# A graph network's layer-1 tables, made block by block beside layer 0's edge loop

## Chip, cores and metric

One core of one Trainium2 chip. The metric is the device time of one execution in microseconds; the kernel before took 9594.02 us, the median of three runs.

## What is computed

Four graph layers with residuals on 12500 nodes of 128 features and 200000 edges. dst is sorted; it is drawn as 12500 u², so low nodes have most of the edges. h is the rectified layer norm of x ahead of every layer.

```python
# layer 0: attention over incoming edges and a self loop, at dst
h = h @ W; e = leaky_relu(a_s[src] + a_d[dst])
x = x + segment_sum(h[src] * softmax_by_dst(e), dst)
# layer 1: 8 heads, at src
q, k, v = h @ Wq.T + bq, h @ Wk.T + bk, h @ Wv.T + bv
a = (dot(q[src], k[dst]) / 4 + mlp(edge_weight1)) * cutoff(edge_weight1)
x = x + layernorm(h + segment_sum(softmax_by_src(a) * v[dst], src) @ Wo.T + bo)
# layer 2: both directions, normed by degree; layer 3: mean over dst, batch norm
```

## The kernel before

The nodes are 98 blocks of 128. Edges are handled 128 to a tile; a row gather (`gather`, L340, an indirect DMA issued by GpSimd) fetches one table row for each of a tile's edges, and a one-hot matrix product adds the rows to the sums in SBUF (`acc`, one row of 137 columns per node). There are four stages of gathers: `hw` (layer 0), `kvt` (layer 1), `zt` (layer 2), `h` (layer 3).

`layer0_edges` is unrolled in 196 steps. A step takes two windows of four tiles: eight gathers, then the weights of the edges (L1346 to L1358), the weighted one-hot matrices on ScalarE and VectorE (L1365 to L1368), four matmuls per window (L1372), and two additions per window into the two blocks that a window can touch (L1375). Because dst is sorted, low blocks are complete long before the loop ends. A generator, `background`, is advanced once a step, and twice in every sixteenth: it loads layer 1's weights and then sorts the edges by source (`sort`; L484 to L497 are its exchanges, L518 to L529 its turns through PE).

After the loop, the sorted keys are stored to DRAM, `layer0_wide` stands as a loop that runs 0 times or once (a test of the data, read into a register by every engine, decides; it doesn't run here), and then comes the stage between the layers. It works in seven chunks of 14 blocks: `layer0_out` divides by the sums and adds x (L1463), `layernorm_stats` takes statistics (L313), the result goes to DRAM (`xd`), `layer1_table` makes keys, values and queries (a rectified norm L329, a transpose L777, its copy L779, two matmuls of 384 columns L1476 and L1477, three copies out L1478 to L1480) and stores them (`kvt`, `qd`). Between chunks `source_tiles` makes layer 1's lists: for each tile the indices, places and lengths of its edges, with 2 + 13 + 13 gathers from the sorted keys (`edge`, `keyt`, `far`), unpacking on VectorE (L442 to L449) and 39 transposes (L1221). `cutoff` follows. All kvt rows must be in DRAM before layer 1's first gather.

Layer 1's loop (`attention`) has its order written out by hand, as a pipeline over groups of eight tiles. Layer 2 (`layer2_edges`) mixes gathers with sums by buckets of edges, which need the array `bucketp`, loaded by `bucket_places`. Elsewhere the framework's scheduler chooses each engine's order ahead of time; engines then run in that order and wait on semaphores.

```python
for lo, hi in groups(c0, c1):
    net.layer1_table(work, psum2, kv_view, q_view, rows0, lo, hi, ln)
nc.gpsimd.memset(acc[:, c0:c1, :], 0.0)
for _ in range(2):
    next(fill, None)
```

Of the kernel before, what the change touches and what calls it, by code (L numbers as in the profile page):

```python
# [37 lines left out]
P = 128  # L38
# [19 lines left out]
G = 4  # L58
# [40 lines left out]
CHUNKS = [(b, b + CHUNK) for b in range(0, NB, CHUNK)]  # L99

# [17 lines left out]
class Net:  # L118
# [773 lines left out]
    def bucket_places(self, pool, places, over):  # L892

        nc = self.nc
        place = pool.tile([P, BC, P], F32, name="bucketp")
        nc.sync.dma_start(place, places)
        none = pool.tile([P, 1], F32, name="bnone")
        nc.vector.tensor_scalar(none, over, -4096.0, None, op0=OP.mult)
        nc.vector.tensor_scalar(place, place, none, None, op0=OP.add)
        return place.rearrange("p c b -> p (c b)")  # L900

    def buckets(self, work, psum, table, lanes, place, finish, classes=CLASSES, zb=ZB):
# [15 lines left out]
        for k0 in range(0, classes, n):  # L918
            cols = COLS[k0 // FEW]
            sums = [psum.tile([P, 512], F32, name=f"sums{i}", bufs=1)[:, :cols] for i in range(n)]  # L920
            for s in range(NB):
# [10 lines left out]
                for i in range(0, n, 2):  # L932
                    p = psum.tile([P, 2, PARTS * D], F32, name="pout", bufs=2)
                    yours = work.tile([P, 2, COLS[classes > FEW]], F16, name="yours", bufs=4 + (zb == ZB))[:, :, :cols]
                    for j in range(2):
                        b = s * CLASSES + k0 + i + j
                        nc.tensor.matmul(p[:, j, :], mine[:, (i + j) * P:(i + j + 1) * P], z[:, s % zb, :],  # L937
                                         start=True, stop=True)
                        nc.vector.tensor_scalar(yours[:, j, :], self.iotac[:, :cols], place[:, b:b + 1], None,  # L939
                                                op0=OP.is_equal)  # L940
# [57 lines left out]
    def windows(self, pool, psum, dram, lists, own, other, rel, size, count, lanes):  # L998
# [9 lines left out]
        ownf = pool.tile([P, RC, P], F32, name="ownf")  # L1008
# [22 lines left out]
        for i, e in enumerate((P - 1, (E - 1) % P)):  # L1031
# [4 lines left out]
        some = pool.tile([P, 2], F32, name="somefar")  # L1036
# [4 lines left out]
                                       self.ident[:, last % P:last % P + 1], op0=OP.is_ge, op1=OP.mult)  # L1041
        p = self.bank(psum)
        nc.tensor.matmul(p[:, 0:2], self.ones, some, start=True, stop=True)
        nc.vector.tensor_scalar(self.found[size], p[:, 0:2], 0.5, None, op0=OP.is_gt)

        nc.vector.tensor_sub(rel, ownf, base[:, :, None].to_broadcast([P, RC, P]))
        otherf = pool.tile([P, RC, P], F32, name="otherf")
# [37 lines left out]
    def source_tiles(self, pool, psum, dram, lists, keys, shifted, values, firsts, lanes, lengths):  # L1085
# [9 lines left out]
        idx, place, void, length, oblocks, obases = lists  # L1095
# [5 lines left out]
        f = small("firsts", R)  # L1101
# [32 lines left out]
        below = small("below", R, BF16)  # L1134
# [60 lines left out]
        key = pool.tile([P, RC, P], I32, name="keyt")  # L1195
        far = pool.tile([P, RC, P], F32, name="far")
# [8 lines left out]
        own, other, rest = (pool.tile([P, RC, P], I32, name=f"{n}t") for n in ("own", "other", "rest"))  # L1205
# [6 lines left out]
        short = pool.tile([P, RC, P], F16, name="shortt")  # L1212
# [3 lines left out]
        for c0 in range(0, RC, 4):  # L1216
            n = min(4, RC - c0)
            for i, (t, out) in enumerate(((otherf, idx), (rel, place), (far, length))):
# [8 lines left out]
            yield  # L1227
        nc.vector.tensor_scalar(void, place, float(P), -1e30, op0=OP.is_ge, op1=OP.mult)
        yield

    def source_pairs(self, pool, key, sown, sother):

        nc = self.nc
        keys, own, other, more = (pool.tile([P, RC, P], I32, name=f"{n}p") for n in ("key", "own", "other", "more"))
        nc.vector.memset(keys[:, RC - 1, :], 0)
        self.load_rows(keys, key)
        self.unpack_buckets(own, other, more, keys)
        self.store_rows(sown, own)
        self.store_rows(sother, other)
        first = pool.tile([P, RC], F32, name="firstp")  # L1240
        nc.vector.memset(first, float(NOWHERE))
        whole = R - (RC - 1) * P
        nc.vector.tensor_copy(first[:, :RC - 1], own[:, :RC - 1, 0])
        nc.vector.tensor_copy(first[:whole, RC - 1:], own[:whole, RC - 1, 0:1])
        return sown, sother, first
# [79 lines left out]
    def layer0_edges(self, acc, lists, background):  # L1325
        nc, tc = self.nc, self.tc
        idx, place, mask, blocks, bases = lists
        n = D + 2
        with tc.tile_pool(name="l02", bufs=1) as work, tc.tile_pool(name="ps02", bufs=2, space=PSUM) as psum:
            self.banks = 2  # L1330
            steps = background(psum)
            for s in range(-(-NW // 2)):
                lo, two = s * W, min(2, NW - 2 * s)
                m = two * G
                rows = work.tile([P, W, ROW], F32, name="rows", bufs=5)
                for j in range(m):
                    self.gather(rows[:, j, :], self.hw, idx, lo + j)
                lane = work.tile([P, W * P], BF16, name="lanes", bufs=3)
                nc.sync.dma_start(lane[:, :m * P], self.rows(self.dlanes[lo:lo + m, :], m * P))
                near = work.tile([P, 2, 3], BF16, name="near", bufs=4)  # L1340
                for i, v in enumerate(self.blocks_of(bases, 2 * s, two, [SP], NP - P - 1)):
                    nc.sync.dma_start(near[:, i, :], self.tb[bass.ds(v, P), :])
                b = self.blocks_of(blocks, 2 * s, two, [DVE], NB - 2)

                mine = work.tile([P, W, P], BF16, name="mine", bufs=2)
                nc.vector.tensor_scalar(mine.rearrange("p g e -> p (g e)")[:, :m * P], lane[:, :m * P], self.lane, None,  # L1346
                                        op0=OP.is_equal)
                pt = psum.tile([P, W, 3], F32, name="pt")
                for j in range(m):
                    nc.tensor.matmul(pt[:, j, :], mine[:, j, :], near[:, j // G, :], start=True, stop=True)  # L1350
                w = work.tile([P, W], F32, name="weight", bufs=3)
                nc.vector.tensor_reduce(w[:, :m], pt[:, :m, :], axis=AX.X, op=OP.add)
                nc.vector.tensor_mul(w[:, :m], w[:, :m], rows[:, :m, D + 2])
                nc.vector.tensor_max(w[:, :m], w[:, :m], rows[:, :m, D + 3])
                minus = work.tile([P, W], F32, name="minus", bufs=3)
                nc.vector.tensor_scalar(minus[:, :m], w[:, :m], -1.0, None, op0=OP.mult)  # L1356

                nc.vector.reciprocal(rows[:, :m, D + 1], w[:, :m])  # L1358
                hot = work.tile([P, W, P], F32, name="weights", bufs=2)
                for j in range(m):  # L1360
                    at = place[:, lo + j:lo + j + 1]
                    if j % G < 3:

                        off = work.tile([P, P], BF16, name="off", bufs=8)
                        nc.scalar.activation(off, self.iotab, AF.Abs, bias=at, scale=-1.0)  # L1365
                        nc.scalar.activation(hot[:, j, :], off, AF.Relu, bias=w[:, j:j + 1], scale=minus[:, j:j + 1])  # L1366
                    else:
                        nc.vector.tensor_scalar(hot[:, j, :], self.iota, at, w[:, j:j + 1], op0=OP.is_equal, op1=OP.mult)  # L1368
                for i in range(two):
                    p = psum.tile([P, n], F32, name="psum", bufs=2)  # L1370
                    for j in range(i * G, i * G + G):
                        nc.tensor.matmul(p, hot[:, j, :], rows[:, j, :n], start=j % G == 0, stop=j % G == G - 1)  # L1372
                    d = acc[:, bass.ds(b[i], 2), :n]
                    for h in range(2):
                        nc.vector.scalar_tensor_tensor(d[:, h, :], p, mask[:, 2 * s + i, h:h + 1], d[:, h, :], op0=OP.mult,  # L1375
                                                       op1=OP.add)
                next(steps, None)
                if s % 16 == 8:
                    next(steps, None)
            for _ in steps:  # L1380
                pass
            self.banks = 1
# [74 lines left out]
    def layer0_out(self, acc, rden, x, lo, hi):  # L1457
# [3 lines left out]
        nc.vector.reciprocal(rden[:, lo:hi], acc[:, lo:hi, D])  # L1461
        for b in range(lo, hi):
            nc.vector.scalar_tensor_tensor(acc[:, b, :D], acc[:, b, :D], rden[:, b:b + 1], x[:, b - lo, :],  # L1463
                                           op0=OP.mult, op1=OP.add)

    def layer1_table(self, work, psum, kv_view, q_view, x, lo, hi, ln):

        nc = self.nc  # L1470
        kv = work.tile([P, 4, 2 * D], F32, name="kv", bufs=2)
        q = work.tile([P, 4, 2, D], F16, name="qparts", bufs=2)
        ht = self.normed_transposed(work, psum, x, lo, hi, ln)
# [908 lines left out]
```

## Time and profile before

| | us |
|---|---|
| timed runs, median (lowest, highest) | 9594.02 (9591.22, 9601.5) |
| profiled execution, its own time | 7967.66 |
| its span | 7965.0 |
| layer 0's edge loop, first to last gather | 196.4 to 2168.1 |
| layer 1's gathers begin | 2346.4 |
| layer 2's gathers begin | 4750.8 |
| layer 3's gathers begin | 7048.7 |
| mean granted TensorE clock | 0.759 |

The profile is of one execution. Its time is shorter than that of the timed runs; the profile does not say why. A group's line gives the line of code, the engine, the operation, what is written from what, the shapes and the count; then the busy time and the mean duration in ns; then the idle time ahead of it on its engine, and what ended most of that. A window's line gives each engine's busy time in a stretch.

### The profile page before, as it was taken

The numbers are of one execution on the slowest core, as the hardware profiler recorded it, in microseconds if no ns is written. First come the engines' busy times: TensorE is split into PE (matmuls) and PEld (weight loads), VectorE is DVE, ScalarE is ACT, GpSimd is POOL, SyncE is SP. The second block draws the span as 40 slices with busy tenths as digits, with TensorE's granted clock in tenths as the row PEclk, the third lists the DMA queues.
The fourth block names the chain that finished last, engine by engine and source line by source line (L and its number), as shares of the span: only waits on it lengthen the run. The fifth ranks groups of instructions, "written<-read, shape, count | busy, mean of one in ns | idle before, by whom it ended". The sixth has DMA issues, their size and how long they took to land. (4 is left out here: it accounts for less than half of the span.)

```text
span 7965.0 us, 123010 instructions
## 1 busy us (share of the span) xinstructions
PE 5216.0 (65%) x36039; PEld 4233.1 (53%) x36040; DVE 5606.0 (70%) x17675; ACT 3772.7 (47%) x8051; POOL 5505.8 (69%) x5641
## 2 busy tenths in 40 slices
PE   4344544444376666666666537776888898768887
PEld 3344444444346666656666536555644554456665
DVE  5687777777667776666666666666766776778887
ACT  4466666666463333223333364443534454456556
POOL 0777777777637777777777557777777766357774
PEclk7566666656586667677676669888988998879999
DMA  6333333333475555555556514443433443445554
GB/s 107 85 83 82 79 83 80 84 79 82 94 222 186 186 185 175 174 175 172 183 179 189 137 61 135 133 127 118 149 115 118 125 132 117 109 120 135 150 150 122
DMA packets 780792, 1038.72 MB, mean 130 GB/s; under 512 B 202181, under 2 KB 548698, under 8 KB 779834
## 3 DMA queue, kind: packets, MB, share of 16 engines
q1 hardware_dynamic: 535039, 543.32, 23.2%
q0 software_dynamic: 202304, 471.89, 22.1%
q10 hardware_dynamic: 42747, 15.32, 0.9%
q8 instruction: 298, 4.88, 0.2%
q14 instruction: 404, 3.31, 0.1%
HBM read 963.63 MB, written 66.40 MB: 129 GB/s over the span
## 5 line engine op out<-in xcount | busy, mean ns | idle before, releaser
L942 ACT ACTIVATE r<-pout 128x512 f16<-128x512 f32 x2352 | 1400.2, 597 | 1268.9 <-PE pout L937 1144.7
L340 POOL DMA_INDIRECT rows<-hw,idxd x1564 | 1492.5, 954 | 674.1 <-issue 449.0
L340 POOL DMA_INDIRECT rows<-zt,idxs x1624 | 1560.0, 961 | 559.2 <-issue 405.0
L340 POOL DMA_INDIRECT rows<-kvt,idxs x1624 | 1591.3, 980 | 494.9 <-issue 418.5
L914 PE MATMUL sums<-yours,r 128*128 128x288 f16 (+1 forms) x9408 | 1875.9, 323 | 3.2 <-DVE yours L939 2.8
L939 DVE TENSOR_SCALAR yours<-iotac,bucketp 128x288 f16<-128x288 f16 (+1 forms) x4704 | 1351.0, 329 | 311.8 <-PE sums L914 286.1
L1372 PE MATMUL psum<-rows,weights 128*128 128x130 f32 x3128 | 731.6, 415 | 638.0 <-ACT weights L1366 526.9
L914 PEld LDWEIGHTS <-r 128*128 128x128 f16 x9408 | 944.5, 101 | 338.5 <-issue 7.0
L1372 PEld LDWEIGHTS psum<-rows,weights 128*128 128x128 f32 x3128 | 658.0, 311 | 676.6 <-ACT weights L1366 587.7
L937 PE MATMUL pout<-z,mine 128*128 128x256 f16 x4704 | 930.3, 281 | 39.2 <-ACT r L942 35.7
L340 POOL DMA_INDIRECT rows<-h,late x620 | 606.8, 979 | 185.4 <-issue 145.5
L1602 ACT ACTIVATE weighted<-lg 128x64 f32<-128x64 f32 x203 | 53.1, 262 | 1438.5 <-DVE lg L1600 1438.5
L1623 PE MATMUL psum<-weighted,hot 128*128 128x137 f32 x3136 | 662.6, 391 | 74.4 <-DVE weighted L1612 73.8
L1596 DVE TENSOR_TENSOR rows<-pq,rows 128x512 f32<-128x512 f32 x406 | 280.5, 691 | 571.0 <-DMA rows<-kvt,idxs 570.4
L1623 PEld LDWEIGHTS psum<-weighted,hot 128*128 128x128 f32 x3136 | 622.4, 290 | 98.6 <-DVE weighted L1612 95.2
L1366 ACT ACTIVATE weights<-off,weight,minus 128x128 f32<-128x128 bf16 x1173 | 483.6, 481 | 336.8 <-DVE minus L1356 202.5
L1583 PE MATMUL pq<-query,mine 128*128 128x128 f16 x3136 | 333.7, 291 | 467.5 <-DVE mine L1552 464.7
L1872 PE MATMUL psum<-rows,hot 128*128 128x128 f16 x3248 | 341.8, 232 | 411.8 <-DMA rows<-zt,idxs 367.4
L937 PEld LDWEIGHTS <-mine 128*128 128x128 f16 x4704 | 450.1, 101 | 272.9 <-issue 54.6
L1583 PEld LDWEIGHTS <-mine 128*128 128x128 f16 x3248 | 306.1, 137 | 498.7 <-DVE mine L1552 495.5
L1870 DVE TENSOR_SCALAR hot<-iotac,places 128x128 f16<-128x128 f16 x1624 | 367.6, 281 | 280.4 <-PE psum L1872 279.1
L1872 PEld LDWEIGHTS <-hot 128*128 128x128 f16 x3248 | 249.8, 103 | 528.9 <-issue 475.0
(497 smaller groups left out, 9240.7 us busy)
## 6 DMA issues: line engine op xcount, KB each, us to landing
near<-lengths SPq DMA_DIRECT2D x203, 512.0 KB
lanes<-lanes SPq DMA_DIRECT2D x112, 896.0 KB
lanes<-slanest SPq DMA_DIRECT2D x203, 256.0 KB
z<-zt SPq DMA_DIRECT2D x112, 448.0 KB
lanes<-lanes SPq DMA_DIRECT2D x196, 256.0 KB
lanes<-dlanes SPq DMA_DIRECT2D x195, 256.0 KB
rows<-kvt,idxs POOLq DMA_INDIRECT x1624
rows<-zt,idxs POOLq DMA_INDIRECT x1624
```

What stands on the lines that cost most here:

```text
L340: self.nc.gpsimd.indirect_dma_start(out=out, out_offset=None, in_=table, in_offset=bass.IndirectOffsetOnAxis(ap=idx[:, t:t + 1], axis=0))
L914: nc.tensor.matmul(sums[i], self.part(r[:, i, :], h), yours[:, i, :], start=s == 0 and h == 0, stop=s == NB - 1 and h == PARTS - 1)
L937: nc.tensor.matmul(p[:, j, :], mine[:, (i + j) * P:(i + j + 1) * P], z[:, s % zb, :], start=True, stop=True)
L939: nc.vector.tensor_scalar(yours[:, j, :], self.iotac[:, :cols], place[:, b:b + 1], None, op0=OP.is_equal)
L942: nc.scalar.activation(r, p, AF.Copy)
L1366: nc.scalar.activation(hot[:, j, :], off, AF.Relu, bias=w[:, j:j + 1], scale=minus[:, j:j + 1])
L1372: nc.tensor.matmul(p, hot[:, j, :], rows[:, j, :n], start=j % G == 0, stop=j % G == G - 1)
L1583: nc.tensor.matmul(pq[:, j, :], s["mine"][i][:, j, :], s["query"][i * G + j][:, h * D:(h + 1) * D], start=h == 0, stop=h == 1)
L1596: nc.vector.tensor_mul(k, s["pq"][i], k)
L1623: nc.tensor.matmul(p, s["hot"][j // G][:, j % G, :], v[:, j, :], start=first and j == 0, stop=last and j == W - 1)
L1870: nc.vector.tensor_scalar(hot, self.iotac[:, :P], place[:, lo + j:lo + j + 1], None, op0=OP.is_equal)
L1872: nc.tensor.matmul(p, hot, self.part(rows[:, j, :], h), start=first and h == 0, stop=last and h == PARTS - 1)
```

## The change

- `layer0_out`, `layer1_table` and the chunk loop between the layers become one generator, `layer1_tables`, in chunks of seven blocks (the last two of four and three). `layer0_edges` calls `prep(s)` at the end of every step; it advances the generator by up to two pieces (three once `background` is used up), if `after_step` says that the chunk's blocks are complete by that step. What is left runs after the loop. acc is no longer cleared afterwards, and x + layer 0's output stands in the chunk's own tile.
- A test in `windows` compares, for each chunk but the last, the first dst of the row at which the chunk is due with the chunk's end. If some block is late (`soon`), a loop after layer 0 makes all tables again; it runs 0 times or once.
- `background` goes on after the sort with the stores of the keys, `source_tiles` and `cutoff`, and is advanced a second time in every sixth step instead of every sixteenth.
- Memory: five SBUF buffers of 128 x 1664 (`bufs`) serve in turn the edge arrays, the sort, the lists, and later `bucketp`. In `layer0_edges` the small product `pt` has four places in one PSUM bank (two banks before), the two windows' products share one bank in each of two buffers (one bank each before), and the tables get one bank (`prep`). In `attention`, `near` has three buffers instead of four and is loaded three groups ahead instead of four; `weighted` has two instead of three.

```diff
+STEP = 7
+PREP = [(b, b + STEP) for b in range(0, NB - STEP, STEP)] + [(NB - STEP, NB - 3), (NB - 3, NB)]
+def after_step(hi):
+    return min(-(-NW // 2), int(NW * math.sqrt(min(1.0, hi * P / N)) / 2) + 2)
...
+        for i, (_, hi) in enumerate(PREP):
+            row = min(2 * after_step(hi), NW) * G
+            if hi == NB or row >= NW * G:
+                nc.vector.memset(some[:, 2 + i:3 + i], 0.0)
+            else:
+                nc.vector.scalar_tensor_tensor(some[:, 2 + i:3 + i], ownf[:, row // P, 0:1], float(hi * P),
+                                               self.ident[:, row % P:row % P + 1], op0=OP.is_lt, op1=OP.mult)
...
-                pt = psum.tile([P, W, 3], F32, name="pt")
+            pt = pts[:, s % 4]
...
-                    p = psum.tile([P, n], F32, name="psum", bufs=2)
+            p = psum.tile([P, 2, n], F32, name="psum", bufs=2)
...
-                if s % 16 == 8:
-                    next(steps, None)
+            if next(steps, self) is self or s % 6 == 1 and next(steps, self) is self:
+                self.banks = 1
+            prep(s)
...
+    def layer1_tables(self, work, psum, acc, ln, views):
+        for c0, c1 in PREP:
+            yield c1
+            k = c1 - c0
+            x = work.tile([P, STEP, D], F32, name="x", bufs=2)[:, :k]
+            self.load_x(x, c0, c1)
+            rden = work.tile([P, STEP], F32, name="rden", bufs=2)[:, :k]
+            nc.vector.reciprocal(rden, acc[:, c0:c1, D])
+            for b in range(k):
+                nc.vector.scalar_tensor_tensor(x[:, b, :], acc[:, c0 + b, :D], rden[:, b:b + 1], x[:, b, :],
+                                               op0=OP.mult, op1=OP.add)
+                if b % 3 == 2:
+                    yield c1
+            nc.scalar.dma_start(xd_view[:, c0:c1, :], x)
+            self.layernorm_stats(work, ln, c0, c1, x)
+            yield c1
+            for lo in range(0, k, 4):
...
+                for j in range(n):
+                    p = bank()[:, :3 * D]
+                    nc.tensor.matmul(p, self.onesb, self.parts, start=True, stop=False)
+                    nc.tensor.matmul(p, ht[:, j, :], self.qkv, start=False, stop=True)
+                    nc.scalar.activation(q[:, j, 0, :], p[:, :D], AF.Copy)
+                    nc.vector.tensor_sub(q[:, j, 1, :], p[:, :D], q[:, j, 0, :])
+                    nc.scalar.activation(kv[:, j, :], p[:, D:], AF.Copy)
+                    if j % 2:
+                        yield c1
...
+        yield from net.source_tiles(sort_pool, psum, bufs, short, oblocks, obases, skeys[:R, :], shifted, shiftedl,
+                                    firsts, net.by_tile[1], net.by_tile[0])
+        net.cutoff(flat[2], flat[4].bitcast(I32), flat[1])
...
+        def prep(s):
+            for _ in range(2 + (net.banks == 1)):
+                if due and s >= after_step(due[0]) and due[0] < NB:
+                    due[:] = [v for v in [next(tables, None)] if v is not None]
...
+    nc.vector.tensor_max(wide, wide, net.soon)
+    once = net.count_of(dlist, wide, 1)
+    with tc.tile_pool(name="l1t", bufs=1) as work, tc.tile_pool(name="ps10", bufs=1, space=PSUM) as psum, \
+            tc.For_i(0, once, 1):
+        for _ in net.layer1_tables(work, psum, acc, ln, views):
+            pass
```

## The prediction

> **What bounds the kernel now.** I read the page first, then busy time by stage, then GpSimd's timeline where layer 0 ends, then groups of instructions and waits. The page has a group that repeats in all four layers, the row gathers on GpSimd:
>
> ```profile
> L340 POOL DMA_INDIRECT rows<-hw,idxd x1564 | 1492.5, 954 | 674.1 <-issue 449.0
> ```
>
> Its median is 944 ns and 0.30 us of issue stands ahead of each, so a gather costs 1.25 us. Busy time by stage (time, PE, PE's weight loads, VectorE, ScalarE, GpSimd, then clock and DMA):
>
> ```profile
> 200.00:2160.00 1960.00, 881.05 (x5375) 798.51 (x5375) 1422.56 (x3345) 1174.44 (x2902) 1482.95 (x1557) 0.62 0.37 83
> 2160.00:2350.00 190.00, 123.35 (x482) 72.23 (x482) 116.00 (x459) 117.47 (x358) 52.13 (x49) 0.83 0.62 189
> 2350.00:4500.00 2150.00, 1447.40 (x9949) 1390.98 (x9949) 1440.89 (x3680) 672.86 (x1446) 1639.12 (x1671) 0.70 0.59 182
> ```
>
> In layer 0's edges, 1557 gathers x 1.25 = 1946 of 1960 us: GpSimd never stops, and PE (45%), VectorE (73%) and ScalarE (60%) have room. A step is eight gathers, 10.0 us. The second stage, between the edge loops, is the one that the change attacks. GpSimd's timeline shows its edges:
>
> ```profile
> 2167.16 0.94 POOL L340 DMA_INDIRECT rows<-hw,idxd  x1 [0.30 <-issue]
> 2179.63 0.13 POOL L1104 IOTA least<- 128x2 int32 x1 [11.53 <-DVEq L1391]
> 2195.98 1.12 POOL L340 DMA_INDIRECT edge<-skeys,counti  x1 [15.92 <-DVE counti L1140]
> ...
> 2218.51 1.00 POOL L340 DMA_INDIRECT keyt<-skeys,posi  x1 [13.43 <-DVE st L313]
> ...
> 2345.79 0.15 POOL L810 IOTA bnum<- 128x25 int32 x1 [13.64 <-DMA kvt<-kv]
> 2346.44 0.98 POOL L340 DMA_INDIRECT rows<-kvt,idxs  x1 [0.49 <-issue]
> ```
>
> From the end of the last layer-0 gather (2168.1) to the first of layer 1 (2346.4) are **178.3 us**; what ends the wait is the last table block's landing (kvt). Layer 1 is again paced by its gathers, so what is saved here reaches the end.
>
> [...] with VectorE 73% busy, the median gather stays at 944 ns. [...] Before, each product has its own bank [...]; the change puts two in one. [...] VectorE's last addition ends at 2178.5, its next instruction starts at 2182.4.
>
> **The change, part by part.** *(1) The gap.* The table work of 98 blocks goes beside layer 0's steps from 54 on, except for what is left when the loop ends. Block chunks are due at steps 54, 76, 92, 106, 119, 130, 140, 150, 159, 167, 175, 183, 190 and 194 (of 0 to 195), the last three blocks after the loop. A chunk of seven takes nine calls, two to a step, so 84 to 91 runs in 190 to 194, and three calls remain for 91 to 95: four blocks' projections and the last chunk are left. Before, the last scatter ends 10.4 us after the last gather. Then I sum, from rows of the old stage, the last three blocks: reciprocal 0.23 and three updates at 345 ns, 1.3; statistics 2.0; square root 0.31 plus a table load of 1.28, then 0.4, 2.0; three activations at 504 and their transposes 2.2; copy 0.5; first projection (340 + 2 x 526) 1.4 and its three copies 1.0; two further projections 2.8; semaphore hops, my allowance, 3. That is 16 us; the four projections left over add 4. The first loop's skip costs 4 (above). The second loop is new: a maximum and a count at 0.15 each, register loads and a skip; at the first's price plus 2 to 4 I take 7 (bounds 4 and 12). The table's store (2.3 to 2.7 us for zt<-parts) lands under the skips. So 10 + 16 + 4 + 4 + 7 = 41, say 42, against 178.3: **-136 us** (gap from 30 to 70: -148 to -108).
>
> *(2) Moved gathers.* The lists by source bring 2 + 13 + 13 gathers and three small iotas onto GpSimd's queue, ahead of layer-0 gathers in a stage where that queue is the path: 28 x 1.25 + 0.5 = **+35 us**. The seven memsets of acc (1.7 us each) vanish; they hid beside tables: 0. *(3) Their waits.* In the old stage they stood 15.9 and 13.4 us for counti and posi. Now a stop would hold every gather behind it. The old layer-0 order lets VectorE wait for rows (333 us between 300 and 2160), so a gather queued behind several others probably finds its index ready: **+8** (0 to 30).
>
> *(4) Room on the other engines.* VectorE's part, by rows: 98 x (345 + 287 + 278) ns = 89; chunk statistics and reciprocals 15 x 1.6 = 24; list work and cutoff 34; together 147 us. These durations overlap: in 400 to 1200 rows add up to 719 where the windows' union is 609, so 125 us, over 142 steps 0.89 us each. The sort, 443 of those 719, is squeezed: extra turns every sixth instead of every sixteenth step, 1.167/1.0625, +9.8% of 4.5 us, 0.44. VectorE goes from 7.26 to 8.6 us of a 10.0 us step. ScalarE gains 45.3 + 35.6 + 27.5 + 15.7 + 11 = 135, 0.95 a step: 6.9. PE gains 86 + 33 + 22 + 8 = 149, 1.05 a step: 5.5. All fit on average; each seven-block chunk comes in a burst of five steps, and five row buffers cushion some 40 us. I take **+15** for bursts (0 to 45). SP gets 15 loads and 56 stores more at 0.33 us or so, in 142 steps of 10 us: 0. DMA gains 6.4 + 6.4 + 12.8 + 6.4 = 32 MB over 1420 us, 23 GB/s on top of 83, where layer 1 runs at 182: 0.
>
> *(5) Layer 1.* near is loaded three instead of four groups ahead with three buffers; in the timeline its load is issued at 3003.4, just as PE's product frees a buffer, and its own tanh runs three groups later, some 33 us. One group less leaves 22. weighted's two buffers: the exponential writes at 3016.4 what PE's sums left a group earlier. 0 (to +10). *(6) Layer 2.* bucketp is loaded at 4750.0, used at 4768.8. It now goes into buffers free since attention's end and can be loaded earlier, but may share the start with x<-xd: **-6** (-14 to +2). *(7) The test:* some 16 tiny VectorE operations before layer 0 at 0.15: +2, inside the allowance of (4). The work loop itself does not run: after_step leaves a margin of one to two steps, 1024 edges or more, and the standard deviation of a count of 200000 draws is at most 224.
>
> Sum: -136 + 35 + 8 + 15 - 6 = **-84 us**. The profiled execution took 7967.66 us with a span of 7965.0, so 7881 after. The timed runs' median is 9594.02, 1626 us or 1.204 times more, and nothing in the trace says where that lies. Taken over unscaled: 9594 - 84 = **9510 us**; scaled it would be 9493.
>
> **The rivals.** *A, slower: VectorE takes over layer 0.* The two window products of a step now share a bank. If their order alternates (four matmuls, two VectorE additions, four matmuls, two additions), VectorE stands for 4 x 0.415 = 1.66 us in each step. Its room in late steps is 10.0 - 8.6 = 1.4; waits for PE already take (77.9 + 38.7)/186 = 0.63; the new subtraction waiting on ScalarE's copy, at the old 41.6/98 per block, takes 0.29. That leaves 0.49, so the step grows by 1.17, over 142 steps +166 in place of the +15. Span +67: **9661**. It decides from 0.70 us a step up (99/142), a VectorE wait of 1.2. Against it: other VectorE work can be ordered between the two halves. *B, no change: the gap moves.* A tail of 70, the list gathers waiting 30, bursts 45, the layer-2 gain gone: -108 + 35 + 30 + 45 + 2 = +4, or with half the bursts -18: about **9585**. For it: the last two steps carry cutoff and a Sin table load too. *C, clean:* -148 + 35 - 14 = -127, scaled by 1.204 -153: **9441 to 9467**. *D:* the late loop runs after all and repeats the tables, about 140 us: 9650; by the margin above under 1%.
>
> **From cases to numbers.** Main case 0.55 (9470 to 9570), C 0.15, B 0.12, A with D 0.18. 0.2%, 19 us, is about what a measurement of this kernel tells from no change. Faster 0.70, same 0.12, slower 0.18. The range runs from 9450, which keeps most of C, to 9625, between B and A; about 0.17 lies outside. The main case alone: 9470 to 9570.
>
> **What would show it.** Right: layer-0 steps still 10.0 us apart with 0.30 us of issue before most gathers; keyt and far gathers among them at 1.25; first kvt gather 35 to 50 us after the last hw gather; that first kvt gather near 2168 + 35 + 23 + 42 = 2268 instead of 2346. Wrong: GpSimd's gathers in layer 0 released by PE or by landed rows for tens of us, above all after step 54; VectorE waiting on PE psum for over 200 us instead of 78; a kvt group in layer 1 slower than before; a gap above 70.

## The result and the profile after

| | median us | lowest to highest | executions |
|---|---|---|---|
| before | 9592.62 | 9591.22 to 9601.5 | 4 |
| after | 9901.61 | 9891.25 to 9904.44 | 4 |

The changed kernel takes 1.0318 times as long, with an interval of 1.03 to 1.0336: 309 us more where 84 less were predicted. To understand the numbers below one has to know that the chips used were in one of two conditions, which the kernel before tells apart: in **A** it takes 7939 to 7968 us (the profile before is from A), in **B** 9557 to 9609 (the timed runs and the profile after are from B).

The page of the changed kernel has, for the group shown before of layer 0's gathers:

```profile
L350 POOL DMA_INDIRECT rows<-hw,idxd x1564 | 1494.9, 956 | 1110.2 <-PE psum L1390 464.4
```

A gather is as short as before (956 ns). The idle time ahead of them has gone from 674 to 1110 us, and what ended most of it is no longer issue (449 of 674), but PE's product in the sums (464). Busy time of the same three stages, layer 0, the gap, layer 1:

```profile
210.00:2815.00 2605.00, 1060.06 (x5737) 877.32 (x5737) 1510.09 (x3747) 1273.02 (x3186) 1518.51 (x1589) 0.58 0.31 74
2816.00:2875.00 59.00, 35.12 (x116) 22.44 (x116) 23.77 (x102) 30.41 (x80) 0.26 (x1) 0.67 0.23 69
2880.00:5655.00 2775.00, 1565.05 (x9811) 1468.63 (x9811) 1394.85 (x3610) 664.78 (x1421) 1625.52 (x1670) 0.63 0.45 141
```

No engine is full any more in layer 0: GpSimd is busy 58% (76% before), VectorE 58%. Layer 1, which has the same work as before, is 2775 us long instead of 2150. The gap has shrunk as intended, as GpSimd's timeline shows: 59 us in place of 178.

```profile
2815.31 0.94 POOL L350 DMA_INDIRECT rows<-hw,idxd  x1 [0.30 <-issue]
2875.24 0.96 POOL L350 DMA_INDIRECT rows<-kvt,list  x1 [58.98 <-issue]
```

GpSimd's waits in layer 0 (what it waited for: us in total, times, longest), of the changed kernel:

```profile
POOL rows L350 <- PE psum L1390: 464.4, 87, 12.9
POOL rows L350 <- issue: 422.0, 1375, 1.1
POOL rows L350 <- PE pt L1368: 76.7, 15, 12.6
POOL rows L350 <- remote: 68.1, 31, 6.8
```

and in layer 1:

```profile
POOL rows L350 <- DVE weighted L1657: 649.9, 98, 14.7
POOL rows L350 <- issue: 488.3, 1410, 59.0
```

The same waits in the profile before, first layer 0, then layer 1:

```profile
POOL rows L340 <- PE psum L1372: 7.9, 26, 0.3
```

```profile
POOL rows L340 <- DVE weighted L1612: 4.0, 13, 0.3
```

A gather overwrites a tile of rows that an earlier one filled. Here GpSimd stands ahead of it, in layer 0 for PE's products, which read such a tile (464 us), in layer 1 for the weighted rows that VectorE makes of one (650 us). That is the first of the signs that the prediction named as wrong. But the two profiles are from different conditions, so they do not yet tell what the change did.

### The profile page after: what moved, and what is told of

Its sections match the earlier page's. It is cut to its first block, busy times and chain, and to the rows that moved or that the text cites. A ratio compares the mean times of both kernels' runs of the same rounds, so it can differ in the third digit from the quotient of the medians.

```text
span 9900.0 us, 122999 instructions
## 1 busy us (share of the span) xinstructions
PE 5607.6 (57%) x36039; PEld 4400.8 (44%) x36040; DVE 5585.5 (56%) x17758; ACT 3754.7 (38%) x8059; POOL 5481.6 (55%) x5634
## 3 DMA queue, kind: packets, MB, share of 16 engines
q1 hardware_dynamic: 535311, 543.32, 18.5%
## 5 line engine op out<-in xcount | busy, mean ns | idle before, releaser
L350 POOL DMA_INDIRECT rows<-kvt,list x1624 | 1582.9, 975 | 1186.9 <-DVE weighted L1657 649.9
L350 POOL DMA_INDIRECT rows<-zt,list x1624 | 1567.6, 965 | 1126.3 <-issue 414.0
L929 PE MATMUL sums<-yours,r 128*128 128x288 f16 (+1 forms) x9408 | 1944.2, 332 | 17.1 <-issue 11.9
L954 DVE TENSOR_SCALAR yours<-iotac,list 128x288 f16<-128x288 f16 (+1 forms) x3136 | 900.2, 331 | 685.9 <-PE sums L929 261.1
L952 PEld LDWEIGHTS <-mine 128*128 128x128 f16 x4704 | 458.9, 102 | 1129.5 <-issue 905.9
L1621 PE MATMUL pb<-we,near 128*128 128x16 f32 x3248 | 575.6, 292 | 660.1 <-issue 655.6
L1621 PEld LDWEIGHTS pb<-we,near 128*128 128x128 f32 x3248 | 590.2, 253 | 674.7 <-issue 664.3
L1393 DVE SCALAR_TENSOR_TENSOR acc<-psum,mask,acc 128x130 f32 x782 | 269.4, 344 | 733.7 <-remote 505.8
L1915 DVE TENSOR_SCALAR hot<-iotac,list 128x128 f16<-128x128 f16 x1624 | 362.1, 275 | 374.9 <-remote 153.0
L954 DVE TENSOR_SCALAR yours<-iotac,bucketp 128x288 f16<-128x288 f16 x1568 | 415.7, 306 | 187.0 <-PE sums L929 92.4
```

The costliest lines, as they stand in the source:

```text
L350: self.nc.gpsimd.indirect_dma_start(out=out, out_offset=None, in_=table, in_offset=bass.IndirectOffsetOnAxis(ap=idx[:, t:t + 1], axis=0))
L929: nc.tensor.matmul(sums[i], self.part(r[:, i, :], h), yours[:, i, :], start=s == 0 and h == 0, stop=s == NB - 1 and h == PARTS - 1)
L1393: nc.vector.scalar_tensor_tensor(d[:, h, :], p[:, i, :], mask[:, 2 * s + i, h:h + 1], d[:, h, :], op0=OP.mult, op1=OP.add)
L1621: nc.tensor.matmul(pb[:, j].rearrange("p a h -> p (a h)"), s["near"][:, j * P:(j + 1) * P], self.we.rearrange("p a h -> p (a h)"), start=F ...
L1915: nc.vector.tensor_scalar(hot, self.iotac[:, :P], place[:, lo + j:lo + j + 1], None, op0=OP.is_equal)
```

## The experiments

All kernels of one batch ran on one chip, with the kernel before beside them. At first the question was which part of the change costs 309 us; the theories were thin buffers in layer 1, the work put beside layer 0, and the products that share a bank. The first batch fell into condition A.

**1. The kernel before, for its trace.** No edit.

> The kernel before, unchanged, for a second profile. If the timed runs of before stop in the way that the profile after shows (PE, then GpSimd standing for it), this profile has a span near 9590 us, layer-0 gathers over some 2400 to 2500 us and layer-1 gathers over some 2500 to 2700 us instead of 1971 and 2151. If the slower stages come from the change alone, its stages are those of the first profile, with a span near 7965 us.

Measured 7967.69 us, with the stages of the first profile. So the slower stages do not come from the change alone: the 1626 us between the first profile and the timed runs belong to the condition that the chip was in (each chip on record was in one alone), and what follows has to be read for each condition apart.

**2. Layer 1's buffers alone**, in the kernel before:

```diff
-            s["near"] = work.tile([P, W * P], F32, name="near", bufs=4)
+            s["near"] = work.tile([P, W * P], F32, name="near", bufs=3)
...
-            v = s["weighted"] = weighted[g % 3]
+            v = s["weighted"] = weighted[g % 2]
...
-        for i in range(-4, NV + 1):
-            step(load, i + 4)
+        for i in range(-3, NV + 1):
+            step(load, i + 3)
```

> Before, with layer 1's buffers of the change alone: near three deep and loaded three groups ahead, weighted two deep. Theory 'thin buffers' (the loss lies in layer 1): slower by 200 to 350 us. Theory 'layer 0' (the loss lies in layer 0's loop, by the added work or the shared banks): within 20 us of before.

Measured 7959.48, ratio 0.9999 [0.999, 1.0008]. **3. Layer 0's places in PSUM alone**:

```diff
+            pts = psum.tile([P, 4, W, 3], F32, name="pt", bufs=1)
...
-                pt = psum.tile([P, W, 3], F32, name="pt")
+                pt = pts[:, s % 4]
...
+                pp = psum.tile([P, 2, n], F32, name="psum", bufs=2)
...
-                    p = psum.tile([P, n], F32, name="psum", bufs=2)
+                    p = pp[:, i, :]
```

> Before, with layer 0's PSUM layout of the change alone: the two windows' products in one bank, the four small products in one bank. Theory 'shared banks' (my rival A): slower by 150 to 400 us. Theories 'thin buffers' and 'added work': within 30 us of before.

Measured 7967.18, ratio 1.0007 [0.9999, 1.0016]. **4. The changed kernel with all tables after layer 0's loop**, the lists beside it:

```diff
-            for _ in range(2 + (net.banks == 1)):
+            for _ in range(0):
```

> The changed kernel, but all tables are made after layer 0's loop; the lists by source stay beside the loop. Theory 'added work' (the tables beside layer 0 slow its steps by more than they save): faster than the changed kernel by 100 us or more, 9650 to 9800. Theories 'thin buffers' and 'shared banks': slower than the changed kernel by the tables' time, 100 to 200 us, so 10000 to 10100.

Measured 8033.34, ratio 1.0091 [1.0074, 1.0108]. The expected losses were written for B, which this batch did not meet. In A neither the buffers nor the banks cost anything that can be measured, and without the tables beside the loop the changed kernel is 74 us slower than the kernel before: the gap is 203 us, and layer 0, with the moved list gathers in it, takes 2014.

**5. to 7. The changed kernel itself, without the lists beside the loop, and with neither.** This batch fell into B.

> The changed kernel itself, once more. Theory 'the chip': in the condition in which the kernel before takes 7959, GpSimd still paces all stages, and the steps of my sum hold: 7959 - 84 = about 7875 (7840 to 7910), ratio 0.985 to 0.994; the 1.03 belongs to the condition in which the kernel before takes 9592, and comes back only there (9850 to 9950). Theory 'the change': what is put beside layer 0 costs more than it saves anywhere: ratio 1.02 to 1.035 in either condition, that is 8120 to 8240 beside 7959. In the first case the first kvt gather is near 2260, in the second the last hw gather comes after 2450.

```diff
         yield
+
+    def make_lists(psum):
         yield from net.source_tiles(sort_pool, psum, bufs, short, oblocks, obases, skeys[:R, :], shifted, shiftedl,
                                     firsts, net.by_tile[1], net.by_tile[0])
         net.cutoff(flat[2], flat[4].bitcast(I32), flat[1])
...
         net.layer0_edges(work, psum, acc, lists, background, prep)
+        rest = make_lists(psum)
         for _ in tables:
+            next(rest, None)
+        for _ in rest:
             pass
```

> The changed kernel, with the lists by source and cutoff made after layer 0's loop again, between what is left of the tables; the tables stay beside the loop. By my steps 2 and 3 the loop is 35 to 43 us shorter than in the changed kernel, but the lists then stand after it: a gap of some 110 to 150 us instead of 42. Theory 'the chip': where the kernel before takes 7959, about 40 to 70 us above the changed kernel; where it takes 9592, the changed kernel less what the lists cost there, ratio to before 1.01 to 1.03. Theory 'the change': if it is the lists' 28 gathers on GpSimd's queue that stop layer 0, at least 150 us below the changed kernel.

Run 7 has this edit and that of run 4.

> The changed kernel with both the tables and the lists made after layer 0's loop; its buffers, its places in PSUM, its extra turns of the sort in every sixth step and its second, skipped loop stay. Theory 'the chip': layer 0 as before, the gap 180 to 220 us, in all 10 to 45 us above the kernel before, in either condition (ratio 1.001 to 1.006); the changed kernel's loss of 1.03 is then the work beside the loop. Theory 'the change': if it is the buffers or the turns of the sort, 1.02 or more remains.

Measured, beside 9580.26 of the kernel before: the changed kernel 9893.67, ratio 1.0328 [1.0314, 1.0342]; without the lists 9911.71, 1.0341 [1.0323, 1.0358]; with neither 9987.61, 1.0428 [1.0412, 1.0444]. The theory that the work beside layer 0 is what costs 309 us falls: with it taken out, the kernel is 94 us slower still, where by that theory a ratio of at most 1.006 was expected; without the lists alone, 1.01 to 1.03 was expected and nothing is gained. So something that all three kernels share loses most of the 309 us. (The 94 us are no gain over the kernel before: the stage between the layers takes 251 us in run 7 and 182 in the kernel before.)

**8. to 11. Traces and buffers.** Run 8 is the kernel before, run 9 that of run 2 again; runs 10 and 11 are the changed kernel with near's four buffers and its load four groups ahead, and with three buffers of weighted (both together were not run). This batch fell into A.

> The kernel before, for its trace. Where it takes 9580 to 9600 us, its stages tell where the changed kernel's 309 us and the 408 us of e2_neither come from, since those two have the same stages but for layer 0. Theory 'layer 0': the kernel before has layer 1 in about 2780 us and layer 2 in about 2690, as the changed kernel has, and a layer 0 of at most 2200. Theory 'thin buffers': its layer 1 takes 2400 to 2500, about 300 less, and its layer 0 is within 100 of e2_neither's 2509. Where it takes 7960, the stages are 1974, 2152, 2120 and 823 as before.

> The kernel before with layer 1's buffers of the change alone (near three buffers and three groups ahead, weighted two). Where the kernel before takes 9580 to 9600, theory 'thin buffers': 9850 to 10000, most of the loss; theory 'layer 0': no change within 0.3%. Where it takes 7960: no change, as measured before (0.9999).

> The changed kernel with near's four buffers and its load four groups ahead, as in the kernel before; weighted keeps two. Where the kernel before takes 9580 to 9600, theory 'thin buffers' with near as the place: 9580 to 9650 in place of 9894; with weighted as the place, or theory 'layer 0': 9880 to 9910. Where it takes 7960: about 7875, as my sum has it for the changed kernel.

> The changed kernel with three buffers of weighted, as in the kernel before; near keeps three buffers and three groups. Where the kernel before takes 9580 to 9600, theory 'thin buffers' with weighted as the place: 9500 to 9650 in place of 9894 (PE's sums of a group may then lag a group more before the exponential waits for them); with near as the place, or theory 'layer 0': 9880 to 9910. Where it takes 7960: about 7875.

Measured: the kernel before 7940.21 in the one profiled run (7945.45 in the runs beside); with the thinner buffers 7948.05, ratio 1.0004 [0.9995, 1.0013]; the changed kernel with near's buffers 7864.16, **0.9898** [0.9881, 0.9914]; with weighted's 7856.2, **0.9888** [0.9871, 0.9904]. As the buffers have no measurable effect in A by themselves (0.9999 and 1.0004), these two stand for the changed kernel, which was not run in A unaltered: 81 and 89 us faster, where 84 were predicted.

**12. and 13. The kernel before and its thinner buffers, in B.**

> The kernel before, for its trace where it takes 9580 to 9600. Theory 'deep buffers absorb': with PE standing still for 10 to 16 us at a time there, the deeper buffers of layer 1 let the gathers run on: layer 1 in 2450 to 2550 us instead of the changed kernel's 2781, fewer than 300 us of gathers waiting for the weighted rows (652 in the changed kernel), and a layer 0 of at most 2450. Theory 'layer 0': layer 1 in 2770 to 2790, layer 2 in 2690, and layer 0 in at most 2200. Where the kernel takes 7950 this run tells nothing new.

> The kernel before with layer 1's thinner buffers of the change alone, once more, for the condition in which the kernel before takes 9580 to 9600. Theory 'deep buffers absorb': 9850 to 9900 (most of the 309 us of the changed kernel, and three quarters of e2_neither's 408), its layer 1 in 2781. Theory 'layer 0': within 0.3% of the kernel before. Where the kernel before takes 7950: no change (0.9999 and 1.0004 measured).

Measured 9577.55 in the one run (9565.11 beside), and 9763.97, ratio **1.0202** [1.0183, 1.0222]. This is the missing trace. The starts of the first and the last gather of each layer give its stages (us, one profiled execution each):

| | layer 0 | to layer 1 | layer 1 | layer 2 | layer 3 |
|---|---|---|---|---|---|
| A: before (run 8) | 1969 | 178 | 2146 | 2112 | 816 |
| A: changed, weighted back (run 11) | 2008 | 53 | 2140 | 2110 | 817 |
| B: before (run 12) | 2368 | 182 | 2605 | 2675 | 960 |
| B: before, thin buffers (run 13) | 2372 | 181 | 2769 | 2688 | 959 |
| B: changed (run 5) | 2606 | 53 | 2781 | 2692 | 958 |
| B: changed, no lists (run 6) | 2590 | 92 | 2780 | 2691 | 967 |
| B: changed, neither (run 7) | 2509 | 251 | 2782 | 2684 | 961 |

The buffers cost 164 us in layer 1 in B (of 199 in all, by the medians), and nothing measurable in A. The 9764 are less than the 9850 to 9900 that the theory of deep buffers gave, and the kernel before has layer 1 in 2605 and not in 2450 to 2550. The other theory wanted a layer 0 of at most 2200 in the kernel before, and it takes 2368. So both places lose: the change 176 us in layer 1 and 238 in layer 0.

What differs in layer 1 in B is PE. Its products for the weights of edges (L1576), in the kernel before, first in A and then in B:

```profile
L1576 PE MATMUL pb<-we,near x3088: 232/263/376, 2405.6 to 4444.4; 128*128 128x16 f32 x193
its engine sat idle before it (us, times) until:
  issue: 1.9, 2
```

```profile
L1576 PE MATMUL pb<-we,near x3169: 176/263/394, 2749.8 to 5325.9; 128*128 128x16 f32 x199
its engine sat idle before it (us, times) until:
  issue: 1080.3, 955
```

The median of one is the same 263 ns; but ahead of weight loads and products 1080 us of standing are counted in B with nothing recorded that ended them (the two run beside each other, and their idle times are added up here; ahead of the products alone it is 522). Records of releasers are missing in B (the profile after holds 55,530 updates of semaphores, the profile before 154,605), so this alone would not show that PE waited for nothing. The timeline of the sums' weight loads shows it better. Sixteen of them in A (run 8) stand in one row, and in B (run 12) come one by one, 0.70 us from start to start, while the trace gives the last three of these four no semaphore to wait for:

```profile
3235.40 3.16 PEld L1623 LDWEIGHTS psum<-weighted,hot 128*128 128x128 f32 x16
```

```profile
3236.99 0.29 PEld L1623 LDWEIGHTS psum<-weighted,hot 128*128 128x128 f32 x1 [0.41 <-issue]
3237.69 0.29 PEld L1623 LDWEIGHTS psum<-weighted,hot 128*128 128x128 f32 x1 [0.42 <-issue]
3238.40 0.28 PEld L1623 LDWEIGHTS psum<-weighted,hot 128*128 128x128 f32 x1 [0.42 <-issue]
3239.09 0.29 PEld L1623 LDWEIGHTS psum<-weighted,hot 128*128 128x128 f32 x1 [0.40 <-issue]
```

GpSimd stands longer too, in the kernel before as well. Its waits in layer 1 of run 12, and then of run 13:

```profile
POOL rows L340 <- DVE weighted L1612: 493.7, 100, 12.5
POOL rows L340 <- issue: 430.4, 1411, 0.7
```

```profile
POOL rows L340 <- DVE weighted L1612: 649.6, 97, 13.8
POOL rows L340 <- issue: 423.5, 1389, 0.4
```

Under 300 us of this wait were expected in run 12, and it has 494. The thin buffers add 156 us to it, nearly all of the 164. In layer 0 of run 12 a piece of the timeline shows the lag itself:

```profile
1542.64 3.68 PE L1372 MATMUL psum<-rows,weights 128*128 128x130 f32 x16 [6.84 <-ACT bank L484]
1546.21 0.34 DVE L1375 SCALAR_TENSOR_TENSOR acc<-psum,mask,acc 128x130 f32 x1
1554.95 0.35 DVE L1375 SCALAR_TENSOR_TENSOR acc<-psum,mask,acc 128x130 f32 x1 [7.47 <-remote]
1555.18 0.94 POOL L340 DMA_INDIRECT rows<-hw,idxd  x1 [3.22 <-remote]
```

The products end by the record at 1546.3, and the addition that reads them starts at 1555.0, 8.6 us later; a gather then stands for 3.2 us. "Remote" is what the profile says where it finds no releaser in the program; in B many records of releasers are missing. In layer 0 of run 12, 72 additions start more than 2 us after the last product on record, with VectorE idle ahead of them; in run 8 it is 8.

**14. to 16. The turns of the sort, the banks again, and a mended version.** Turns: in the kernel before,

```diff
-                if s % 16 == 8:
+                if s % 6 == 1:
```

The mended version is run 11's kernel with each window's product in a bank of its own:

```diff
-            p = psum.tile([P, 2, n], F32, name="psum", bufs=2)
             for i in range(two):
+                p = psum.tile([P, n], F32, name="psum", bufs=2)
                 for j in range(i * G, i * G + G):
-                    nc.tensor.matmul(p[:, i, :], hot[:, j, :], rows[:, j, :n], start=j % G == 0, stop=j % G == G - 1)
+                    nc.tensor.matmul(p, hot[:, j, :], rows[:, j, :n], start=j % G == 0, stop=j % G == G - 1)
...
-                    nc.vector.scalar_tensor_tensor(d[:, h, :], p[:, i, :], mask[:, 2 * s + i, h:h + 1], d[:, h, :],
+                    nc.vector.scalar_tensor_tensor(d[:, h, :], p, mask[:, 2 * s + i, h:h + 1], d[:, h, :],
```

> The kernel before with the change's places in PSUM in layer 0's loop alone (pt four places in one bank, both window products of a step in one bank). Where the kernel before takes 9565 to 9600, its layer 0 takes 2368 and e2_neither's 2509, with the sums' products released late. Theory 'shared banks': layer 0 in 2460 to 2510, in all 9660 to 9720. Theory 'turns': within 0.3% of the kernel before. Where it takes 7950: no change (1.0007 measured).

> The kernel before with a second turn of the sort in every sixth step in place of every sixteenth, nothing else. Where the kernel before takes 9565 to 9600: theory 'turns': 100 to 140 more, 9660 to 9710; theory 'shared banks': within 0.3%. Where it takes 7950: no change within 0.2%, since VectorE's extra 0.44 us a step has room there.

> The changed kernel with two parts as in the kernel before: each window's product in a PSUM bank of its own (two buffers), and three buffers of weighted; near keeps three, and pt its one bank. Where the kernel before takes 9565 to 9600 and the changed kernel 9894: if weighted is the place in layer 1 and the shared bank the one in layer 0, 9570 to 9640; if only weighted is, 9690 to 9730; if neither, 9880 to 9900. Where the kernel before takes 7950: 7850 to 7870, as with weighted alone (7856).

The batch fell into A: banks 7954.32, ratio 1.0007 [0.9998, 1.0016]; turns 7949.21, 1.0003 [0.9994, 1.0011]; the mended version 7855.92, 0.9881 [0.9865, 0.9898]. For the open question in B they tell nothing; the turns of the sort cost nothing measurable in A. So the mended version was run alone, **17.**, and fell into A again (7863.24, 0.9877 [0.986, 0.9893]), and once more, **18.**, and fell into B.

> The same kernel as e5_after_fix, once more, for the condition in which the kernel before takes 9565 to 9600. There the changed kernel's layer 0 takes 2606 us and its layer 1 2781. Theory 'shared banks': layer 0 in 2460 to 2510; theory 'turns': 2590 to 2610, the turns of the sort staying as they are. In layer 1: weighted as the place gives 2600 to 2650, near as the place 2770 to 2790. Together 9570 to 9640 if it is shared banks and weighted, 9880 to 9900 if neither. Where the kernel before takes 7950: 7856, as measured.

> The kernel of e5_after_fix and e6_after_fix a third time, for the condition in which the kernel before takes 9565 to 9600. Layer 0 in 2460 to 2510 if the shared banks lose there, 2590 to 2610 if the sort's turns do; layer 1 in 2600 to 2650 if weighted loses, 2770 to 2790 if near does. Together 9570 to 9640 if it is banks and weighted, 9880 to 9900 if neither. Where the kernel before takes 7950: 7856 to 7863, ratio 0.988.

In B it measured 9759.81, ratio **1.0169** [1.0142, 1.0197], with layer 0 in 2509 and layer 1 in 2774. Both windows in one bank cost 97 us of layer 0 there (2606 to 2509), at the upper end of the 2460 to 2510 that the theory of shared banks gave. The two profiles are from different chips, and executions of this version spread over 48 us, so 97 is no exact price; by the medians the two edits together give back 134. Whether it is the bank itself, or that both windows' products come free together, is not shown. Weighted's third buffer gives back only 7 us, so the 9570 to 9640 expected of both are missed: the place in layer 1 is near's lead (or the two buffers only together; near alone was not run in B). GpSimd's waits in layer 0 of this version,

```profile
POOL rows L350 <- issue: 414.8, 1357, 0.6
POOL rows L350 <- PE psum L1390: 248.9, 56, 10.7
POOL rows L350 <- remote: 155.8, 69, 6.3
```

show less waiting for the products (249 for 464 in the profile after); but some of it is named remote now (156 for 68), so that the two together go from 532 to 405. Layer 1 has 643.6 us of waiting for weighted, as in the changed kernel. A version with near's four groups and a bank for each product was not run; it is the next to try.

## Why the prediction was wrong

Point by point, in us; A is run 11 less run 8, B is run 5 less run 12 (B's two are on different chips in the same condition). The sums of the columns A and B are the differences of the spans, -85 and +303.5.

| step of the prediction | predicted | A | B |
|---|---|---|---|
| ahead of the first gather (test) | (+2, within the +58) | +11.5 | +12.7 |
| layer 0: gathers, their waits, room (2 to 4) | +58 | +39.1 | +238.5 |
| the gap (1) | -136 | -124.9 | -128.7 |
| layer 1 (5) | 0 | -5.8 | +176.3 |
| from layer 1 to layer 2 (6) | -6 | -2.1 | -11.5 |
| layers 2 and 3, end | 0 | -2.7 | +16.2 |

**In condition A the sum holds**, and the signs that it named are there. That -85 meets -84 within 1 us is luck: layer 0 comes out 19 us lower than predicted, the gap and the start 23 higher, and the rest 5 lower. The mechanism, GpSimd's queue as the path and a shorter gap, is as described. GpSimd's waits in layer 0 of run 11:

```profile
POOL rows L350 <- issue: 415.7, 1364, 0.3
POOL rows L350 <- DMA rows<-hw,idxd: 18.7, 58, 1.0
POOL rows L350 <- PE psum L1390: 12.8, 42, 0.3
POOL list L350 <- issue: 7.3, 24, 0.3
```

24 of the 28 list gathers have the 0.3 us of issue ahead of them and no more: they cost 1.25 each (their median in the profile after is 945 ns) and found their indices ready, and layer 0 grew by 39 where 35 is theirs. The waits (+8) and the bursts (+15) were set too high, by 19 together. VectorE's waits for the products are 141 us, under the 200 named. The gap, from the end of the last gather, is 52 instead of 42. Three engines' timelines show why, in run 11:

```profile
2204.08 0.94 POOL L350 DMA_INDIRECT rows<-hw,idxd  x1 [0.30 <-issue]
```

```profile
2231.20 0.35 DVE L1393 SCALAR_TENSOR_TENSOR acc<-psum,mask,acc 128x130 f32 x1
2250.05 0.41 SPq L1527 DMA_DIRECT2D kvt<-kv  x1
2257.35 0.96 POOL L350 DMA_INDIRECT rows<-kvt,list  x1 [52.33 <-issue]
```

The last addition ends 26.5 us after the last gather, not 10.4, which the prediction had left as before; from there to the last store are 18.5 (20 predicted), and the store and the two skips take 7.3 (11 predicted). The first kvt gather starts at 2257, where the prediction named 2268; in run 8 it starts at 2332, so it comes 74 us earlier, where 78 were predicted. Ahead of the first gather the start grew by 11.5 instead of 2. That is not explained; ten profiles of the kernel before and its variants have the first gather between 183.6 and 196.4, ten of the changed kernel and its variants between 195.5 and 207.3.

**What failed** is the last step of the sum: "Taken over unscaled: 9594 - 84". The prediction had seen that the profiled execution was 1626 us shorter than the timed runs, noted that nothing in the trace says where that lies, and still took every term over. Two of its terms rest on what the trace of A shows and B does not have, that GpSimd never stops. In the kernel before in B, GpSimd's waits in layer 0 already include

```profile
POOL rows L340 <- remote: 223.4, 106, 6.0
POOL rows L340 <- PE psum L1372: 187.0, 45, 9.3
```

410 us of 2368, and layer 0 is 399 longer there than in A. There a part of the path goes through PE (187 us by name; the 223 named remote are not told apart), and what the change gave up between PE and GpSimd cost time:

- Step 5, "0 (to +10)" for layer 1's thinner buffers, is +164 by run 13 alone and +176 in the whole change. The sizes from the timeline (22 us of lead left) were those of A.
- Steps 2 to 4, +58 with "+15 for bursts (0 to 45)": layer 0 is +238. Of this about 97 are the shared banks (run 5 to run 18), 80 the tables (run 7 to run 6) and 17 the lists (run 6 to run 5). If these add, some 45 are left for the turns of the sort, pt's four places in one bank and the moved arrays, which were not tried apart in B.

Rival A named the shared bank, with VectorE as the engine that would stand, and +166 over 142 steps; it had the right place in layer 0, for B alone. The price that it gave, four additions in turn with the products, needs no late PE and would have shown in A too, where the bank costs nothing measurable (1.0007 twice, without the tables beside it) and the changed kernel's layer 0 grows by 39 in all. No rival had layer 1 in it. The gap's gain is real in both conditions (-125 and -129). In B the tables and lists take back 97 of it in layer 0 (run 7 to run 5), so the moved work still gains some 30 us over the kernel before. This is outweighed by what the change gives up to make room for it: 176 us in layer 1, and in layer 0 the 141 that are not the moved work's.

In one place the prediction says more than its lines hold: that the median gather "stays" at 944 ns with VectorE 73% busy. They give it at that load alone. The profile after adds a second: in its layer 0, with VectorE 58% busy, the median is 945 ns.

**Not settled:** what makes PE slow in layer 1, and its results late in layer 0, in B; whether near's lead alone turns that into 164 us, and how; and the remaining 45 us of layer 0.

## What to carry to other kernels

When the profiled time and the timed median differ by a fifth, as here, the profile may show another bound than the one that is timed: settle which, or widen the range to both, before any term is added up. A buffer or a bank that was given up to make room cost nothing measurable here where PE was on time (ratios of 0.9999 and 1.0007 in A), and its price could not be read from that trace; price it also for the case that the engine behind it falls some 10 us behind (in B one addition started 8.6 us after its products). An edit that moves work and thins buffers is best taken apart into these two, since in B here the first gained some 30 us and the second, with what came with it, lost some 320.

## What the runs showed of the hardware

In layer 1 in B, PE gives its instructions in steps of 0.70 us, or twice that, for stretches that come back. In the profile after, from 2900 to 5600 us, there are 96 stretches of four or more such steps with less than 1.5 us between them; their median length is 14.0 us, and from the start of one to the next it is 27.1. Counted from start to start of PE's records (weight loads and products) in layer 1, of the kernel before in runs 8 and 12 and of the profiles before and after:

```
                                      0.65 to 0.75 us    1.3 to 1.5 us
A, run 8 (2400 to 4400 us)                          3                1
B, run 12 (2800 to 5300 us)                       768              293
A, profile before (2400 to 4400 us)                 1                0
B, profile after (2900 to 5600 us)               1118              273
```

Of the same distances, taken together, in these two runs, layer 0 has 24 in B and 22 in A, and layer 2 has 118 and 55. So these steps are a sign of layer 1 above all; layers 0 and 2, which are 399 and some 560 us longer in B, are slow there in a way that does not show in these steps, which no run here explains. The granted clock differs little over the run (0.759 in A, 0.725 in B), and the median gather hardly at all (944 to 946 ns in runs 8 and 12). Instruction fetches do not tell the two apart either: the packets of queue 8, 16 KB in the median, took a median of 0.97 us in the profile before (298 packets) and 0.98 in the profile after (299).

The trace of the profile after, from B, also holds fewer records of semaphore updates than that of the profile before, from A: 55,530 against 154,605, for 122,999 and 123,010 instructions. Releasers read "remote" or "issue" more often there. No run here shows why the records are missing, or whether that has to do with the slow PE.
